# Attention steps between dependent hops, relus between projection chunks, and filter loads on another queue, in a four-layer convolution and attention kernel

## The chip, the cores and the metric

The kernel runs on one core of a Trainium2 chip, in one launch. The metric is device microseconds of that core for one execution of the whole program: the median of three runs. The engines are named as the profile names them: PE is TensorE (PEld its weight loads), ACT is ScalarE, DVE is VectorE, POOL is GpSimd and SP is SyncE, which here only issues DMAs.

## The reference

Four layers act on x of shape 4 x 256 x 64 x 64 (images, channels, rows, columns), all in 32-bit floats. Each adds its result to a normalised input:

```python
def _L0_conv_ref(x, ...):                 # non-local block
    xs = conv3x3(x, smooth_w) + smooth_b
    xs = relu(group_norm(xs, gn1_w, gn1_b))           # 8 groups
    g_x, theta_x, phi_x = conv1x1(xs, ...)            # 128 channels each, 4096 tokens
    attn = softmax(einsum('bnc,bcm->bnm', theta_x, phi_x))
    y = einsum('bnm,bmc->bnc', attn, g_x)
    w_y = group_norm(conv1x1(y, w_w, w_b), gn2_w, gn2_b)
    return w_y * 0.1 + xs
def _L1_conv_ref(x, ...):                 # linear attention, 4 heads of 32
    q, k, v = conv1x1(rmsnorm(x), w_qkv)
    q, k = softmax(q, axis=-2), softmax(k, axis=-1)
    context = einsum('bhdn,bhen->bhde', k, v)
    out = einsum('bhde,bhdn->bhen', context, q * scale)
    return rmsnorm(conv1x1(out, w_out) + b_out)
def _L2_conv_ref(x, ...):                 # generated depthwise 3x3 and pointwise kernels
    dk, pk = gen_kernel(x, Wd1, ...), gen_kernel(x, Wp1, ...)
    return pointwise(depthwise3x3(x, dk), pk) + bias
def _L3_conv_ref(x, ...):                 # mixture of four 1x1 experts, gated by the pooled input
    return conv1x1(x, mixture(experts, gate(x)))

for L in (_L0_conv_ref, _L1_conv_ref, _L2_conv_ref, _L3_conv_ref):
    x = x + L(_gn(x))                     # group norm, 32 groups
```

## The kernel before, in words

The 256 channels are two halves (`h`, NH = 2) of 128 partitions; an image's 4096 pixels lie along the free axis, in chunks of CH = 1024 or 512 columns.

**Stages.** The images b = 0 to 3 go through in overlap. The first convolution runs (`convolve_first`), and `project` turns image 0's relu output `big` into phi, theta and g (the tile `tpg`). In stage b, for b = 0, 1, 2, the attention over image b (`attend(b)`) is interleaved with other layers: in stage 0 with the preparation of the convolution's weights and the convolution of image 1 (`convolve_second`), in stages 1 and 2 with all that is left of image b - 1 after its attention (`tail(b - 1)`) and with the convolution of image b + 1 (`convolve`). Then `project` runs for image b + 1, with only the finish of the last attention block beside it. Stage 3 interleaves `attend(3)` with `tail(2)`; `tail(3)` comes last, alone.

**Attention steps.** `attend` has 128 steps per image. One step issues two products of logits (`pf`, L989), their exponentials on ScalarE (`pr`, L990), and two products of the probabilities before it into `py` (L1097); eight matmul instructions of 128 x 512 in all. Logits run one step ahead of the products that use them.

**Chain and credit.** The order on every engine is written out by hand (`manual_schedule`), and each engine works its queue in that order. A layer is a Python generator that issues some instructions and yields a cost n. `Chain.steps` adds n times the stage's rate (1.22 in stage 0, 0.86 in stages 1 and 2, 1.24 in stage 3) to a credit; for each whole unit it lets one attention step be issued and then whatever `w.later` has put off by so many steps. So whether a step falls between two hops of a layer depends on the credit at that point. The final `tail(3)` has a chain of its own (`end`), which draws on work held back for it.

**Hops.** `group_finish` (L339) is the finish of a group norm: statistics on VectorE (`mv`), an averaging matmul (`pm`, L351), `ev` on VectorE, a second matmul (`pv`, L366), then the reciprocal root. It is called in `nonlocal_out`, `input_stats`, `normed_relu`, `linear_attention`, `generated` and `mixed`. `linear_attention` (L1214) scales chunks of its input with `normed` (half 0 on ScalarE, L1234, half 1 on VectorE, L1235), transposes them on TensorE (`turned`, `ps_xt`, L1246), and after its chunks goes through `cx`, `cxT`, `cmT`, `w2`, each a small matmul and a copy. `generated` (L1432) makes the depthwise kernels for the taps on VectorE (L130); `mixed` gates the experts (`ps_hid`, L1708).

**Relus.** `normed_relu` (L666) ends a convolution: `group_finish`, then relu over `big` on ScalarE: eight activations of 128 x 1024 (L687), or for image 1, whose result lies in a planar layout, sixteen of 128 x 512 that read it transposed (L676). Each region is added to `xs_d` in DRAM, which `copy_x` has filled with the input, by an accumulating DMA from GpSimd (`add_by_dma`).

**Filters.** The convolutions are done as products with transformed filters. `load_filter` (L478) fetches one of 256 KB to a `u` tile (three buffers) from `filters` or `rows_d`, one product ahead, all on SyncE's queue; `convolve` makes 24 products per image, `convolve_second` 18 pairs. SyncE also issues the images' loads, `copy_x`, the loads and stores of the attention's results, and the gather of `inv` (L1022).

Of the kernel before, what the change touches and what calls it, by code (L numbers as in the profile page):

```python
# [10 lines left out]
ALU = mybir.AluOpType  # L11
# [35 lines left out]
class Chain:  # L47
# [46 lines left out]
def conv_preact_fast(ctx: ExitStack, tc: tile.TileContext, guard, x, wc, wtpg, ww, wqkv, wout, w1cat, wd2,  # L94
# [244 lines left out]
    def group_finish(st, avg, eps, shift=None, between=()):  # L339

        mv, late = st() if callable(st) else aggregated(st), None
        if isinstance(mv, tuple):
            mv, late = mv
        if shift is not None:
            tt(mv[:, :, 0], mv[:, :, 0], shift, ALU.add)
        yield 1
        pm = bank("pm")  # L350
        nc.tensor.matmul(pm[:, 0:NH], avg, mv[:, :, 0], start=True, stop=True)  # L351
# [12 lines left out]
        yield 1  # L364
        pv = bank("pv")
        nc.tensor.matmul(pv[:, 0:NH], avg, ev, start=True, stop=True)  # L366
# [111 lines left out]
    def load_filter(a, k, last):  # L478

        u = filter_tile("u")  # L480
        nc.sync.dma_start(out=u, in_=rows_d[a, :, :, 0 if k == 0 else 2] if k in (0, last) else filters[a, :, k - 1])
        return u

    def joining(a, y, t):
# [178 lines left out]
        for h in range(NH):  # L663
            nc.sync.dma_start(out=xs_d[b, h], in_=x[b, bass.ts(h, P), :])

    def normed_relu(w, b, st):  # L666
# [4 lines left out]
        if b == 1:  # L671
            for s in range(2):
                tiles = bass.ts(s, IY // 2)
                for h in range(NH):
                    for k in range(MY):
                        nc.scalar.activation(  # L676
                            image[:, h, tiles, k, :].rearrange("p i (t j) -> p i j t", j=MX),
                            outs[:, h, k].rearrange("p j (i t) -> p i j t", t=IX)[:, tiles], AF.Relu,
                            bias=sh[:, h:h + 1], scale=sc[:, h:h + 1])
                        yield 0.5  # L680
                    cols = bass.ts(s, N // 2)
                    w.later(1, lambda h=h, cols=cols: add_by_dma(xs_d[b, h, :, cols], big[:, h, cols]))
            return
        for c in range(N // CH):
            cols = bass.ts(c, CH)
            for h in range(NH):
                nc.scalar.activation(big[:, h, cols], big[:, h, cols], AF.Relu, bias=sh[:, h:h + 1], scale=sc[:, h:h + 1])  # L687
                w.later(1, lambda h=h, cols=cols: add_by_dma(xs_d[b, h, :, cols], big[:, h, cols]))
                yield 0.3

    def convolve(w, b):

# [56 lines left out]
            yield 0.8  # L749
        yield from w.pending()  # L750
        stats(3)
        yield from normed_relu(w, b, st)

    def convolve_second(w):

        _, gm, rstd = yield from input_stats()
        yield from normalise_planar(gm, rstd)
        st = stats_tile()
        products, joined, rows_joined, joining, stats = planar_joiner(st)
        PRODUCTS = [(a, pair) for a in range(TY) for pair in PAIRS]  # L760
# [12 lines left out]
        def join(a, pair, ps):  # L773
            dst = joined(a, pair, ps, False)
            if pair == (3, 4):
                if a == 5:
                    some(len(rest))
                w.later(1, lambda: joined(a, pair, ps, True))
            elif pair == (1, 2):
                pass  # L780
            elif a == 4:

                for oh in range(NH):
                    rest.extend(joining(a, oh, dst[oh]))
                for j in range(4):
                    w.later(1 + j, lambda: some(3))
                for j in range(3):
                    w.later(5 + j, lambda j=j: stats(j))
            elif a == 2:
                for oh in range(NH):  # L790
                    rest.extend(joining(a, oh, dst[oh]))
                for j in range(3):
                    w.later(1 + j, lambda: some(2))
            else:
                some(len(rest))
                for oh in range(NH):
                    w.later(1, lambda oh=oh: rows_joined(a, oh, dst[oh]))

        def load_filters(i):
            a, pair = PRODUCTS[i]  # L800
            return [load_filter(a, k, 5) for k in pair]

        us = load_filters(0)
        copy_x(1)
        for i, (a, pair) in enumerate(PRODUCTS):
            if pair == PAIRS[0]:

                pace = 1.8 if a == 5 else 0.87
                for op, *args in down(a, planar, ra, rt, ra):
                    op(*args)  # L810
                    yield 0.75 * pace
            (v, ops), u = across(pair), us
            if i + 1 < len(PRODUCTS):
                us = load_filters(i + 1)
            for op, *args in ops:
                op(*args)
                yield 0.4 * pace
            w.later(1, lambda a=a, pair=pair, v=v, u=u: multiply(a, pair, v, u))
            yield pace
        yield from w.pending()  # L820
        stats(3)
        yield from normed_relu(w, 1, st)

    def convolve_first(w):

# [90 lines left out]
            tt(mean, mean, minus, ALU.subtract)  # L916
            return mv

        yield from normed_relu(w, 0, moments)


    def project():

        for c in range(N // 512):
# [194 lines left out]
    def nonlocal_out(w, b, big, k4, xs_in):  # L1119
# [94 lines left out]
    def linear_attention(w, b, big, qT, k4, st, sh, sums):  # L1214
# [16 lines left out]
        def normed(c):  # L1231
            cols = bass.ts(c, 512)
            xg = k4("xg").rearrange("p (h n) -> p h n", h=NH)
            nc.scalar.activation(xg[:, 0, :], big[:, 0, cols], AF.Identity, bias=nb[:, 0:1], scale=rstd[:, 0:1])  # L1234
            nc.vector.tensor_scalar(xg[:, 1, :], big[:, 1, cols], rstd[:, 1:2], nb[:, 1:2], ALU.mult, ALU.add)  # L1235
            return xg

        def turned(xg):
# [97 lines left out]
        yield 1  # L1336
# [5 lines left out]
        yield 1  # L1342

        pw = bank("ps_w2")
        nc.tensor.matmul(pw[:, 0:NH * P], cmT, wout_s, start=True, stop=True)
# [3 lines left out]
        yield 1  # L1349

        st = stats_tile()

# [77 lines left out]
    TAPS = [(i, j) for i in range(3) for j in range(3) if (i, j) != (1, 1)]  # L1430

    def generated(w, b, big, k4, st, sh, diag):  # L1432
        mv, gm, rstd = yield from group_finish(st, avg8, 1e-5, sh)

        pivot = sp.tile([P, NH], F32, name="pivot", bufs=1)
# [397 lines left out]
    with tc.manual_schedule(engines={E.PE, E.Activation, E.DVE, E.Pool, E.SP}):  # L1833
        run(Chain(convolve_first).steps())
        run(project())
        for b in range(B - 1):
# [609 lines left out]
```

## Time and profile before

| | |
|---|---|
| median of three runs | 3051.3 us (3050.59 to 3051.98) |
| the profiled execution, own time | 3047.78 us |
| its span | 3045.6 us |
| its mean granted clock | 0.991 |
| PE busy | 2950.2 us, 97% |
| DVE busy | 2062.9 us, 68% |
| ACT busy | 1189.3 us, 39% |
| POOL busy | 130.6 us, 4% |
| attention products (L989 and L1097), PE | 970.8 + 963.5 us |
| DMA moved | 200.55 MB, mean 66 GB/s |

The profile is of one execution. Busy times of the engines overlap. A row of groups has, after the bar, the busy time of all its instructions and the mean of one in ns, then the idle time before them and what ended it. A line of the timeline has the start in us, the duration, the engine, the line of the code, the operation and its tiles, how many instructions it sums (x8), and in brackets the idle time ahead and what ended it.

### The profile page before, as it was taken

How to read it: one execution, taken by the hardware profiler on the slowest of the kernel's cores; microseconds unless marked ns; L12 is line 12 of the kernel's file. 1: busy time of each engine (PE TensorE's matmuls, PEld its weight loads, DVE VectorE, ACT ScalarE, POOL GpSimd, SP SyncE). 2: the span in 40 equal slices, each digit the busy share in tenths (PEclk: the TensorE clock that was granted, in tenths of full speed). 3: DMA queues.
4: the chain of work that ended last, by engine and by line, in shares of the span. 5: the costliest groups of instructions: out<-in, count | busy, mean ns of one | idle time of the engine just before them, and what ended most of it. 6: DMA issues, size and time to landing. Idle time of an engine off the chain costs nothing.

```text
span 3045.6 us, 24705 instructions
## 1 busy us (share of the span) xinstructions
PE 2950.2 (97%) x8562; PEld 1497.6 (49%) x8562; DVE 2062.9 (68%) x2842; ACT 1189.3 (39%) x2295; POOL 130.6 (4%) x178
## 2 busy tenths in 40 slices
PE   6899999999999999999999999999999999999998
PEld 3454555445664444444566444444446544444743
DVE  8747677853646994777545797568554559876584
ACT  2234333353555333223365532412335453333632
POOL 0100000000011000001011000000100100000100
PEclk9999999999999999999999999999999999999998
DMA  5234434352113233532410433333422222234021
GB/s 222 76 104 98 104 55 47 42 70 81 57 8 47 27 76 76 111 52 58 132 7 11 54 20 87 134 50 45 103 84 14 25 42 38 36 90 92 22 69 67
DMA packets 532389, 200.55 MB, mean 66 GB/s; under 512 B 470689, under 2 KB 480673, under 8 KB 528033
## 3 DMA queue, kind: packets, MB, share of 16 engines
q1 hardware_dynamic: 528224, 182.12, 29.2%
q0 software_dynamic: 4032, 16.78, 3.0%
q8 instruction: 69, 1.13, 0.2%
q14 instruction: 64, 0.52, 0.1%
HBM read 130.13 MB, written 85.52 MB: 71 GB/s over the span
## 4 chain that ended last, share of the span: by engine, by line
PE 84%; DVE 8%; issue 5%; DMA 2%; ACT 1%; POOL 0%; SPq 0%; DVEq 0%; POOLq 0%; ACTq 0%
PE pf L989 26%; PE py L1097 26%; PE ps_conv L515 4%; PE ps_tp L929 4%; PE ps_qk L1266 3%; PE ps_ex L1754 3%; PE ps_pw L1532 3%; PE ps_conv L587 2%; PE ps_g L934 2%; PE ps_ctx L1293 2%; PE ps_wy L1041 2%; PE ps_o L1359 2%; PE ps_dw L1579 1%; DVE big L130 1%; DMA u<-filters 1%
## 5 line engine op out<-in xcount | busy, mean ns | idle before, releaser
L990 ACT ACTIVATE pr<-pf 128x512 f32<-128x512 f32 x1024 | 605.2, 597 | 1096.8 <-PE pf L989 1045.5
L989 PE MATMUL pf<-tpg 128*128 128x512 f32 x2048 | 970.8, 597 | 0.0
L1097 PE MATMUL py<-pr,tpg 128*128 128x512 f32 x2048 | 963.5, 593 | 3.8 <-ACT pr L990 3.6
L127 DVE TENSOR_TENSOR tot<-tot,pr 128x1024 f32<-128x1024 f32 x448 | 546.6, 1220 | 225.9 <-ACT pr L990 225.0
L1097 PEld LDWEIGHTS py<-pr,tpg 128*128 128x128 f32 x2048 | 389.8, 190 | 496.7 <-issue 483.0
L989 PEld LDWEIGHTS pf<-tpg 128*128 128x128 f32 x2048 | 385.5, 191 | 432.5 <-issue 411.5
L130 DVE SCALAR_TENSOR_TENSOR dw<-xp,dk,dw 128x1008 f32<-128x1008 f32 x208 | 262.8, 1267 | 6.5 <-ACT dw L1524 3.6
L515 PE MATMUL ps_conv<-v,u 128*128 128x512 f32 x384 | 174.6, 602 | 7.4 <-DMA u<-rows_d 4.6
L515 PEld LDWEIGHTS ps_conv<-v,u 128*128 128x128 f32 x384 | 73.9, 193 | 102.5 <-issue 100.6
L929 PE MATMUL ps_tp<-big,wtpg_s 128*128 128x512 f32 x256 | 117.2, 601 | 3.0 <-ACT big L687 3.0
L127 DVE TENSOR_TENSOR tpg<-ps_g,bg_s 128x512 f32<-128x512 f32 x32 | 22.1, 691 | 143.5 <-PE ps_g L934 143.5
L220 POOL TENSOR_TENSOR rstd<-rstd,half 128x2 f32<-128x2 f32 x24 | 17.5, 729 | 2324.2 <-DVE rstd L368 2207.6
L1266 PE MATMUL ps_qk<-wqkv_s,xg 128*128 128x256 f32 x496 | 113.7, 379 | 0.0
L1266 PEld LDWEIGHTS ps_qk<-wqkv_s,xg 128*128 128x128 f32 x496 | 93.9, 190 | 23.3 <-issue 12.0
L1532 PE MATMUL ps_pw<-dw,pk 128*128 128x512 f32 x216 | 97.4, 592 | 0.0
L930 ACT ACTIVATE tpg<-ps_tp,btp_s 128x512 f32<-128x512 f32 x64 | 43.8, 686 | 116.8 <-PE ps_tp L929 116.6
L1281 DVE TENSOR_REDUCE qs<-qk 128x16 f32<-128x512 f32 x25 | 17.1, 686 | 86.2 <-ACT qk L1276 86.2
L929 PEld LDWEIGHTS ps_tp<-big,wtpg_s 128*128 128x128 f32 x256 | 47.6, 194 | 54.5 <-issue 50.0
L1276 ACT ACTIVATE qk<-ps_qk,rinv 128x256 f32<-128x256 f32 x100 | 47.2, 474 | 67.7 <-PE ps_qk L1266 64.6
L934 PEld LDWEIGHTS ps_g<-wtpg_s,big 128*128 128x128 f32 x512 | 62.2, 192 | 15.3 <-issue 15.3
L127 DVE TENSOR_TENSOR v<-ra 128x1024 f32<-128x1024 f32 x58 | 69.2, 1220 | 0.3
L1762 ACT ACTIVATE res<-ps_ex,b 128x512 f32<-128x512 f32 x56 | 38.1, 687 | 77.8 <-PE ps_ex L1754 75.9
(390 smaller groups left out, 3079.0 us busy)
## 6 DMA issues: line engine op xcount, KB each, us to landing
xp<-in_x_dram SPq DMA_DIRECT2D x16, 1024.0 KB, 8.2
wy_d<-wt SPq DMA_DIRECT2D x32, 512.0 KB, 3.0
wy<-wy_d SPq DMA_DIRECT2D x32, 512.0 KB, 4.9
out_dram<-res SPq DMA_DIRECT2D x64, 256.0 KB, 2.0
xs_d<-big POOLq DMA_DIRECT2D x24, 512.0 KB, 11.9
u<-filters SPq DMA_DIRECT2D x48, 256.0 KB, 3.1
xs<-xs_d SPq DMA_DIRECT2D x24, 512.0 KB, 5.7
u<-rows_d SPq DMA_DIRECT2D x36, 256.0 KB, 3.2
```

What stands on the lines that cost most here:

```text
L127: nc.vector.tensor_tensor(o, a, b, op)
L130: nc.vector.scalar_tensor_tensor(o, a, s, b, op0, op1)
L515: nc.tensor.matmul(ps[oh], u(oh, h), v[:, bass.ts(h, 512)], start=(h == 0), stop=(h == NH - 1))
L587: nc.tensor.matmul(ps[:, bass.ts(oh, IY * IX)], u[i][:, h, bass.ts(oh, P)], v[:, i, bass.ts(h, IY * IX)], start=(h == 0), stop=(h == NH - 1))
L929: nc.tensor.matmul(ps, wtpg_s[:, h, k, :], big[:, h, cols], start=(h == 0), stop=(h == NH - 1))
L934: nc.tensor.matmul(ps[:, j, :], big[:, h, bass.ts(4 * c + j, P)], wtpg_s[:, h, 2, :], start=(h == 0), stop=(h == NH - 1))
L989: nc.tensor.matmul(pf, phi[:, bass.ts(2 * m + s, P)], theta[:, bass.ts(q, 512)], start=True, stop=True)
L990: nc.scalar.activation(pr[:, bass.ts(s, 512)], pf, AF.Exp)
L1097: nc.tensor.matmul(py, g[:, bass.ts(2 * m + s, P)], probs[i][:, bass.ts(s, 512)], start=(m == 0 and s == 0), stop=(m == NM - 1 and s == 1))
L1266: nc.tensor.matmul(ps[:, 0:2 * HID], xg[:, h, bass.ts(j, P)], wqkv_s[:, h, 0:2 * HID], start=(h == 0), stop=(h == NH - 1))
L1532: nc.tensor.matmul(ps, pk[:, h * NH * P + oh * P:h * NH * P + (oh + 1) * P], dw[h][:, bass.ts(s, 512)], start=(h == 0), stop=(h == NH - 1))
L1754: nc.tensor.matmul(ps, wm[h][:, bass.ts(oh, P)], big[:, h, bass.ts(c, 512)], start=(h == 0), stop=(h == NH - 1))
```

## The change

1. A layer may yield `None`. That issues exactly one attention step at that place and takes one from the credit, to which the rate is added: the average pace stays, and the place is fixed. It stands at both hops of `group_finish`, before the `group_finish` of `nonlocal_out` and of `generated` (except in the last tail), before that of the relus in `convolve` and `convolve_second`, after the first relus, between `normed(0)` and the first transposes of `linear_attention` (except in the last tail), and at the four hops from `cx` to the outputs.
2. `normed_relu` cuts its relus in eight pieces (a 1024-column chunk of one half; for image 1 a piece is four activations of 128 x 256). Two run at once. The other six wait in a list, and `project` takes one after each of its 512-column chunks. The accumulating DMA is issued with its piece.
3. `convolve` (images 2 and 3) loads its filters from ScalarE's queue.
4. `convolve_second` loads the first filter of the next pair before, and the second after, the product of a pair.
5. In the last tail, `normed` does half 1 on ScalarE as well for every chunk but the first, and two products instead of one are issued ahead.
6. The rates become 1.34, 0.845 and 1.2.

```diff
@@ Chain.steps
             for n in part:
+                if n is None:
+                    credit += self.rate - 1
+                    yield
+                    self.tick()
+                    continue
                 credit += n * self.rate
@@ group_finish (both hops)
-        yield 1
+        yield None
         pm = bank("pm")
...
-        yield 1
+        yield None
         pv = bank("pv")
@@ load_filter
-        nc.sync.dma_start(out=u, in_=...)
+        (nc.scalar if last == 3 else nc.sync).dma_start(out=u, in_=...)
@@ normed_relu
+    relus = []
+    def normed_relu(b, st, hops=0):
         bias = vec_s[:, V_SB, :]
+        for _ in range(hops):
+            yield None
         _, gm, rstd = yield from group_finish(st, avg32, 1e-5, bias)
         sc, sh = affine(gm, rstd, vec_s[:, V_G1W, :], vec_s[:, V_G1B, :], bias, 1.0)
+        def piece(c, h):
             cols = bass.ts(c, CH)
+            if b == 1:
+                tiles = bass.ts(c, IY // 4)
+                for k in range(MY):
+                    nc.scalar.activation(
+                        image[:, h, tiles, k, :].rearrange("p i (t j) -> p i j t", j=MX),
+                        outs[:, h, k].rearrange("p j (i t) -> p i j t", t=IX)[:, tiles], AF.Relu,
+                        bias=sh[:, h:h + 1], scale=sc[:, h:h + 1])
+            else:
                 nc.scalar.activation(big[:, h, cols], big[:, h, cols], AF.Relu, bias=sh[:, h:h + 1], scale=sc[:, h:h + 1])
-                w.later(1, lambda h=h, cols=cols: add_by_dma(xs_d[b, h, :, cols], big[:, h, cols]))
-                yield 0.3
+            add_by_dma(xs_d[b, h, :, cols], big[:, h, cols])
+        relus.extend(lambda c=c, h=h: piece(c, h) for c in range(N // CH) for h in range(NH))
+        for _ in range(NH):
+            relus.pop(0)()
+        yield None
@@ convolve, convolve_second: the relus' own first None
-        yield from normed_relu(w, b, st)
+        yield from normed_relu(b, st, 1)
@@ convolve_second
-        def multiply(a, pair, v, u):
+        def multiply(a, pair, v, u, after):
             ps = products(pair, v, u)
+            after()
...
-            (v, ops), u = across(pair), us
-            if i + 1 < len(PRODUCTS):
-                us = load_filters(i + 1)
+            (v, ops), u, us = across(pair), us, []
+            load_one(us, i + 1, 0)
...
+            w.later(1, lambda a=a, pair=pair, v=v, u=u, after=lambda us=us, i=i: load_one(us, i + 1, 1): multiply(a, pair, v, u, after))
@@ project, after each chunk
+            if relus:
+                relus.pop(0)()
             yield
@@ nonlocal_out
+        else:
+            yield None
         wmv, gm, rstd = yield from group_finish(wy_stats[b], avg32, 1e-5, bias, between)
@@ linear_attention
-            nc.scalar.activation(xg[:, 0, :], big[:, 0, cols], AF.Identity, ...)
-            nc.vector.tensor_scalar(xg[:, 1, :], big[:, 1, cols], ...)
+            for h in range(NH):
+                if h == 1 and (c == 0 or not alone):
+                    nc.vector.tensor_scalar(xg[:, h, :], big[:, h, cols], ...)
+                else:
+                    nc.scalar.activation(xg[:, h, :], big[:, h, cols], AF.Identity, ...)
...
         xg, first = normed(0), ()
+        if not alone:
+            yield None
         rinv, banks = turned(xg)
         if alone:
-            first = [product(xg, 0)]
+            first = [product(xg, j) for j in range(2)]
...
@@ linear_attention, at each of four hops (cx, cxT, cmT, w2)
-        yield 1
+        yield None
@@ generated
+        if diag is None:
+            yield None
         mv, gm, rstd = yield from group_finish(st, avg8, 1e-5, sh)
@@ the stages
-            run(Chain(both(*parts), 1.22 if b == 0 else 0.86).steps(), attention)
+            run(Chain(both(*parts), 1.34 if b == 0 else 0.845).steps(), attention)
-        run(Chain(tail(B - 2, big, qT, held=held), 1.24).steps(), attention)
+        run(Chain(tail(B - 2, big, qT, held=held), 1.2).steps(), attention)
```

More of the change, by code (lines that the diff above doesn't have):

```diff
@@ L480, in load_filter @@
         u = filter_tile("u")
-        nc.sync.dma_start(out=u, in_=rows_d[a, :, :, 0 if k == 0 else 2] if k in (0, last) else filters[a, :, k - 1])
+        (nc.scalar if last == 3 else nc.sync).dma_start(out=u, in_=rows_d[a, :, :, 0 if k == 0 else 2] if k in (0, last) else filters[a, :, k - 1])
         return u
@@ L664, in copy_x @@
             nc.sync.dma_start(out=xs_d[b, h], in_=x[b, bass.ts(h, P), :])
-    def normed_relu(w, b, st):
+    relus = []
+    def normed_relu(b, st, hops=0):
         bias = vec_s[:, V_SB, :]
+        for _ in range(hops):
+            yield None
         _, gm, rstd = yield from group_finish(st, avg32, 1e-5, bias)
         sc, sh = affine(gm, rstd, vec_s[:, V_G1W, :], vec_s[:, V_G1B, :], bias, 1.0)
[L671 to L681, printed above, removed]
-                    w.later(1, lambda h=h, cols=cols: add_by_dma(xs_d[b, h, :, cols], big[:, h, cols]))
-            return
-        for c in range(N // CH):
-            cols = bass.ts(c, CH)
-            for h in range(NH):
-                nc.scalar.activation(big[:, h, cols], big[:, h, cols], AF.Relu, bias=sh[:, h:h + 1], scale=sc[:, h:h + 1])
-                w.later(1, lambda h=h, cols=cols: add_by_dma(xs_d[b, h, :, cols], big[:, h, cols]))
-                yield 0.3
+        def piece(c, h):
+            cols = bass.ts(c, CH)
+            if b == 1:
[6 more added lines that the diff above has]
+            else:
+                nc.scalar.activation(big[:, h, cols], big[:, h, cols], AF.Relu, bias=sh[:, h:h + 1], scale=sc[:, h:h + 1])
+            add_by_dma(xs_d[b, h, :, cols], big[:, h, cols])
[3 more added lines that the diff above has]
+        yield None
     def convolve(w, b):
@@ L797, in join, with load_one @@
                     w.later(1, lambda oh=oh: rows_joined(a, oh, dst[oh]))
[L799 to L803, printed above, removed]
+        def load_one(us, i, n):
+            if i < len(PRODUCTS):
+                a, pair = PRODUCTS[i]
+                us.append(load_filter(a, pair[n], 5))
+        us = []
+        for n in range(2):
+            load_one(us, 0, n)
         copy_x(1)
@@ L817, in convolve_second @@
                 yield 0.4 * pace
-            w.later(1, lambda a=a, pair=pair, v=v, u=u: multiply(a, pair, v, u))
+            w.later(1, lambda a=a, pair=pair, v=v, u=u, after=lambda us=us, i=i: load_one(us, i + 1, 1): multiply(a, pair, v, u, after))
             yield pace
@@ L821, in convolve_second @@
         stats(3)
-        yield from normed_relu(w, 1, st)
+        yield from normed_relu(1, st, 1)
     def convolve_first(w):
@@ L917, in moments @@
             return mv
-        yield from normed_relu(w, 0, moments)
+        yield from normed_relu(0, moments)
     def project():
@@ L1233, in normed @@
             xg = k4("xg").rearrange("p (h n) -> p h n", h=NH)
-            nc.scalar.activation(xg[:, 0, :], big[:, 0, cols], AF.Identity, bias=nb[:, 0:1], scale=rstd[:, 0:1])
-            nc.vector.tensor_scalar(xg[:, 1, :], big[:, 1, cols], rstd[:, 1:2], nb[:, 1:2], ALU.mult, ALU.add)
+            for h in range(NH):
+                if h == 1 and (c == 0 or not alone):
+                    nc.vector.tensor_scalar(xg[:, h, :], big[:, h, cols], rstd[:, h:h + 1], nb[:, h:h + 1], ALU.mult, ALU.add)
+                else:
+                    nc.scalar.activation(xg[:, h, :], big[:, h, cols], AF.Identity, bias=nb[:, h:h + 1], scale=rstd[:, h:h + 1])
             return xg
@@ L1335, in linear_attention @@
         nc.scalar.copy(cxT, pt[:, 0:NH * P])
-        yield 1
+        yield None
         pe = bank("ps_cm")
@@ L1341, in linear_attention @@
         tt(cmT, pe[:, 0:P], avg32, ALU.mult)
-        yield 1
+        yield None
         pw = bank("ps_w2")
@@ L1348, in linear_attention @@
         w.settle()
-        yield 1
+        yield None
         st = stats_tile()
@@ L1432, in generated @@
     def generated(w, b, big, k4, st, sh, diag):
+        if diag is None:
+            yield None
         mv, gm, rstd = yield from group_finish(st, avg8, 1e-5, sh)
```

## The prediction

> **What bounds the kernel now.** I read the page first, then busy time by stretch, the waits of TensorE by stretch, the timeline around each wait, and the groups.
>
> ```profile
> PE 2950.2 (97%) x8562; PEld 1497.6 (49%) x8562; DVE 2062.9 (68%) x2842; ACT 1189.3 (39%) x2295; POOL 130.6 (4%) x178
> PE   6899999999999999999999999999999999999998
> PEclk9999999999999999999999999999999999999998
> ```
>
> TensorE is busy 97%: only about 95 us of the span are idle, and no matmul is removed. By stretch:
>
> ```profile
> 745.00:1440.00 695.00, 680.70 (x1882) 334.29 (x1881) 495.99 (x659) 274.35 (x534) 34.82 (x41) 0.99 0.30 56
> 1485.00:2180.00 695.00, 680.69 (x1882) 334.43 (x1882) 496.48 (x660) 274.06 (x534) 34.83 (x41) 0.99 0.30 56
> ```
>
> The second number is TensorE's busy time. These are the stages of attention on images 1 and 2 (stages 1 and 2 below), each with 14.3 us idle and the same waits, so every figure for one counts twice. The other stretches: the head to 26 us, 24.6 idle; the first projection, 8.4 (relus, untouched); stage 0 (185 to 745), 0; stage 3 (2224 to 2795), 2.3; the tail after 2795, about 36 with the image-3 layers alone. TensorE's waits from 745 to 1485 (columns: total us, times, longest):
>
> ```profile
> PE pm L351 <- DVE mv L127: 5.3, 3, 3.0
> PE ps_conv L515 <- DMA u<-rows_d: 2.3, 1, 2.3
> PE ps_xt L1246 <- ACT xg L1234: 2.1, 1, 2.1
> PE py L1097 <- ACT pr L990: 1.8, 1, 1.8
> PE ps_conv L515 <- DMA u<-filters: 1.4, 1, 1.4
> PE pv L366 <- DVE ev L127: 0.8, 1, 0.8
> PE ps_w L1345 <- DVE cmT L127: 0.4, 1, 0.4
> ```
>
> The sum is 14.1: this list is what the change can win in a stage. A wait also slows what follows, or doesn't:
>
> ```profile
> 789.78 1.25 PE L1246 MATMUL ps_xt<-ident,xg 128*128 128x128 f32 x8 [2.13 <-ACT xg L1234]
> 790.83 3.46 PE L989 MATMUL pf<-tpg 128*128 128x512 f32 x4
> ...
> 1529.61 1.10 PE L1246 MATMUL ps_xt<-ident,xg 128*128 128x128 f32 x8 [2.13 <-ACT xg L1234]
> 1530.54 1.88 PE L989 MATMUL pf<-tpg 128*128 128x512 f32 x4
> ```
>
> After the same 2.13 us gap four matmuls took 3.46 us once and 1.88 once. That extra (1.58) is the clock.
>
> **Removed, step by step.** One attention step is 3.43 us of TensorE. The hops that now wait had no step between them, or one too early; a demanded step covers any hop in the list, the longest being 2.98.
> - Head of the non-local block, pm 1.58 x 2 = 3.2; generated kernel, pm 0.70 x 2 + 0.19 in stage 3 = 1.6; statistics before the relus, pm 2.98 x 2 = 6.0; input statistics, pv 0.84 x 2 = 1.7. First transposes, 2.13 x 3 = 6.4; context chain (ps_w), 0.38 x 2 = 0.8.
> - Exps behind four relus in a row: 1.81 x 2 = 3.6. Two relus (2.3 us) now stand ahead of them, about what a step leaves ScalarE free (3.43 less two exps of 0.6).
> - Filters: (1.38 + 2.33) x 2 = 7.4. The cause is SyncE's queue (the view after the next sums).
> Idle time: 30.7. Clock: matmuls after these gaps against the undisturbed 1.88 (four) and 3.60 (eight convolution matmuls): 1.58 after the transposes, 1.77 and 1.68 after the filters (5.37 and 5.28), 1.51, 1.88 and 1.02 after the relus' statistics: 9.4.
>
> ```profile
> 1241.87 0.37 SPq L1022 DMA_DIRECT2D inv<-sum_d  x1
> 1242.35 8.62 SPq L481 DMA_DIRECT2D u<-rows_d  x1
> 1254.17 5.37 PE L515 MATMUL ps_conv<-v,u 128*128 128x512 f32 x8 [2.33 <-DMA u<-rows_d]
> ```
>
> The filter's issue stood 8.62 us on SyncE, behind the gather of `inv`; elsewhere an issue takes 0.33 to 0.52 and a filter lands in 3.2 (median). The first wait is a load issued at 1225.86 behind copy_x, 15.3 us to landing. From ScalarE the loads stand behind neither.
>
> In the tail's linear attention both halves of `normed` go to ScalarE after chunk 0, and two products stand ahead:
>
> ```profile
> PE ps_xt L1246 <- DVE xg L1235: 3.9, 2, 2.4
> ```
>
> The two waits are 1.47 and 2.39. VectorE gets 0.54 us back per chunk, ScalarE takes 0.82 more on some 4.9 of a 6.5 us chunk, so it keeps up. I put the first at 0.5 (the second product, two 0.38 matmuls, fills it) and the second at 0: 3.4 won (bounds: -1 to 3.9, if ScalarE were late with its second half).
>
> Gains: 30.7 + 9.4 + 3.4 = 43.5.
>
> **Added.**
>
> ```profile
> L687 ACT ACTIVATE big<-big,sh,sc 128x1024 f32<-128x1024 f32 x24 | 28.0, 1235 | 12.7 <-DVE sh L127 12.7
> L676 ACT ACTIVATE big<-xp,sh,sc 128x512 f32<-128x512 f32 x16 | 19.7, 1312 | 2.9 <-DVE sh L127 2.9
> L1234 ACT ACTIVATE xg<-big,nb,rstd 128x512 f32<-128x512 f32 x24 | 19.6, 816 | 6.1 <-DVE nb L127 5.7
> ```
>
> - Image 1's relus (transposed reads). Contiguous rows give 0.82 ns per element and 0.40 us fixed (816 and 1235 ns); the transposed 512 take 1312. With the fixed part kept, 256 take 0.86 alone; half of 1312 is 0.66; I take 0.77. Two pieces are then eight activations, 6.2 us, ahead of the exps. Four relus of 4.64 us made py wait 1.81, so 6.2 makes it wait 3.4 (2.6 to 4.1). The other six pieces (3.1 each) fall one into each chunk of the projection, which is 5.22 us on TensorE. A piece whose half completes a 1024-column tile is needed two matmul groups later: it is ready about 4.05 after the previous theta activation, TensorE wants it at 2.64: 1.45 x 3 = 4.4 (3.0 to 5.3). Sum 7.8 (5.6 to 9.4). The relus on image 1 were spread over attention steps before, and stage 0 had no wait, so nothing excludes this loss. Images 2 and 3: a piece is 1.15, ready at 2.1 of 2.64, hidden by the projection's matmuls; uncovered it would be 1.2 x 3 per image.
> - A step moves away from one hop. Replaying the credit at both rates, the demanded steps give every listed hop at least one, but in stages 1 and 2 the hop from pv to ps_hid (the experts' gate) falls from one step to none. The nearest row is that wait in the tail, alone:
>
> ```profile
> 3000.44 0.59 PE L1708 MATMUL ps_hid<-rpool,rw_s 128*64 128x1 f32 x4 [1.23 <-DVE rpool L127]
> ```
>
>  TensorE's order is fixed, so the attention's matmuls behind it wait too: 1.2 x 2 = 2.4 (0 to 3).
> - Filter loads on ScalarE: 12 at 0.33 and 12 at 0.52 is 10.2 us a stage, on an engine busy 274 of 695. Behind each stand the next exps, for which TensorE waits; a step has 3.43 - 1.2 = 2.2 us of slack on ScalarE, so one issue hides. The first filter now stands behind the normalising activations, and beside copy_x: 0 to 4.5, and I take 2.0 x 2 = 4.0.
> - Exps behind three of those activations in a row (1.24 each; four of 1.16 cost 1.81): 0.5 x 2 = 1.0 (0 to 1.8).
> - Rate 0.86 to 0.845 gives VectorE more work per step in the depthwise taps, where it is busy 49.4 of 50: 0.5 for both (0 to 2.6). Otherwise the rates cost nothing: steps per image stay 128, and by the replay 126, 126 and 121 are used (124, 127, 120 before). If they ran out, each bare hop would cost 1 to 3.
> - Clock after the new waits, two of them as above: 2 x 1.65 = 3.3 (0 to 6).
> - Accumulating DMAs issued at once on GpSimd (0.88 each, engine 4% busy) are read a stage later: nothing. The second filter of each pair in convolve_second moves behind the multiply; its cover is two attention steps (6.9 us) against 3.2 to land; without it each of 36 loads could cost some us.
>
> Costs: 7.8 + 2.4 + 4.0 + 1.0 + 0.5 + 3.3 = 19.0. Net 43.5 - 19.0 = 24.5. The profiled execution took 3047.8 (span 3045.6), 3.5 under the median of 3051.3; it would become 3023.3, the median **3026.8**.
>
> **Two rules against the trace.** The row: 2.13 us idle, then 3.46 for 1.88. The Trainium skill, "TensorE: Matmul & The Clock Gate", Part 1, "The HAM clock gate", lets the clock drop only after about 3.4 us of idleness. By it no gap here costs clock: gains 34.1, costs 15.7, net 18.4, 3032.9. The trace differs, in five of the gaps; I take the trace, and keep the rule in the range. Second, 8.62 us of held issue. "DMA: Bandwidth & Descriptors", "Issuing engines are not separate DMA queues", says all issuers share the same 16 DMA engines and only issue time is saved. By it the transfers of copy_x and `inv` would delay a filter from ScalarE as well, and 7.4 + 3.45 (their clock) are not won: 24.5 - 10.9 = 13.6, 3037.7. I take the 8.62, which is issue time, but not as certain.
>
> **Rivals.**
> - R1, the costs hide: relus' waits and the first filter prove covered, net about -40, 3011. For: TensorE had no wait in stage 0, with the same relus. Against: eight in a row precede one pair of exps. 0.18.
> - R2, filters gain nothing (the shared engines): 3037.7, as above. For: 15.3 us beside copy_x. Against: 8.62 is issue. 0.20.
> - R3, slower: filter loads hold ScalarE's queue. A load waits for its tile, three of them, while exps stand behind. At 1 us per load, 48 loads make +48: about 3075. It decides at 24.5 / 48 = 0.51 us per load. For: SyncE was held 8.62 once. Against: 2.2 us of slack per step. 0.05.
> - Not doing what it says: where credit already gave a step (stage 0 and 3), a demanded one changes nothing, and the gaps could move to the next hop; no measurable change 0.05.
>
> **How the numbers follow.** The forecast has 0.52; with all costs at their low ends it is 3013, with all at their high ends 3040; they won't all lie on one side, so its own range is 3016 to 3036. Adding R1 and most of R2: 3010 to 3042. This kernel's measurement tells about 0.2%, 6 us. Faster 0.52 + 0.18 + 0.20 = 0.90; within, 0.05; slower, R3, 0.05.
>
> **What would show it.** In stages 1 and 2: pm, ps_xt and py waits gone, TensorE idle near 7 instead of 14.3; a new ps_hid wait of 1.2; no filter issue over 1 us. In the projection of image 1, which ends near 745: ps_tp waiting on relus about 1.45, three times, and py 3.4 before it. Wrong: py waits spread over stages 1 and 2 (R3), or filters still waited for behind copy_x (R2).

## The result, and the profile after

The changed kernel takes 3042.36 us (median of 11 runs, 3041.30 to 3044.86) against 3050.06 for the kernel before in the same runs: a ratio of 0.9978, 95% interval 0.9969 to 0.9987. It is faster by about 7 us; the prediction said 24.5. The profiled execution took 3041.82, 5.96 less than the one before.

The page after, the same three lines:

```profile
PE 2948.7 (97%) x8562; PEld 1496.9 (49%) x8562; DVE 2057.4 (68%) x2835; ACT 1192.6 (39%) x2318; POOL 122.0 (4%) x182
PE   6899999999999999899999999999999999999998
PEclk9999999999999999999999999999999999999999
```

At this resolution nothing has happened but an 8 in one slice, 1216 to 1292 us, where the first of the waits below lies. The stretches of stages 1, 2 and 3 (they start and end at other times now; the second number is TensorE's busy time, the first the length):

```profile
750.00:1437.00 687.00, 675.29 (x1888) 333.04 (x1887) 495.39 (x659) 266.07 (x529) 22.73 (x35) 1.00 0.30 56
1480.00:2172.00 692.00, 680.20 (x1899) 335.83 (x1898) 496.52 (x660) 267.04 (x530) 22.73 (x35) 0.99 0.30 56
2214.00:2786.00 572.00, 569.14 (x1636) 286.22 (x1635) 384.78 (x542) 244.46 (x496) 24.61 (x29) 0.99 0.30 51
```

Stages 1 and 2 still have 11.7 and 11.8 us idle, where 14.3 were before and about 7 were forecast. In the whole execution TensorE's idle time fell from 95.4 to 91.3 us and its busy time by 1.5. The waits of TensorE from 745 to 1485 show that it is other idle time (total, times, longest):

```profile
PE ps_conv L520 <- DMA u<-filters: 7.6, 1, 7.6
PE pm L356 <- DVE mv L132: 2.3, 1, 2.3
PE ps_hid L1730 <- DVE rpool L132: 1.2, 1, 1.2
PE ps_zt L1409 <- DVE z L132: 0.6, 1, 0.6
```

Of the seven waits of before none is left at its place, as forecast. But one filter alone now costs twice what two did, and a hop that had no wait (the group norm ahead of linear attention) has one of 2.3. In the projection of image 1:

```profile
PE ps_tp L940 <- ACT big L686: 2.0, 3, 0.7
PE py L1110 <- ACT pr L1003: 2.0, 1, 2.0
```

The timeline where the 7.6 arises (ACTq is ScalarE's own DMA queue), and the line of the tile's transfers:

```profile
1225.45 1.31 SPq L669 DMA_DIRECT2D xs_d<-in_x_dram  x2
1226.36 0.35 ACTq L486 DMA_DIRECT2D u<-filters  x1
...
1242.81 5.07 PE L520 MATMUL ps_conv<-v,u 128*128 128x512 f32 x8 [7.57 <-DMA u<-filters]
...
DMA to landing us min/median/max: 3.0/7.0/16.3
```

The first filter is issued 0.9 us after the 4 MB of copy_x and lands 16.3 us later. The eight matmuls then take 5.07 instead of 3.60. Before, SyncE's order put the first filter ahead of copy_x, and only the second stood behind; the first product waited for nothing:

```profile
1223.83 0.46 SPq L481 DMA_DIRECT2D u<-filters  x1
1224.34 1.48 SPq L664 DMA_DIRECT2D xs_d<-in_x_dram  x2
1225.86 0.58 SPq L481 DMA_DIRECT2D u<-filters  x1
...
1232.89 3.60 PE L515 MATMUL ps_conv<-v,u 128*128 128x512 f32 x8
```

Stage 3 has a wait that it did not have, and its cause is in these lines:

```profile
2531.23 0.37 SPq L1035 DMA_DIRECT2D inv<-sum_d  x1
2531.64 9.06 SPq L1479 DMA_DIRECT2D wp<-in_wp_dram  x2
...
2544.22 0.75 DVE L135 SCALAR_TENSOR_TENSOR pk<-wp,pb,pk 128x512 f32<-128x512 f32 x1 [11.20 <-DMA wp<-in_wp_dram]
...
2546.20 2.06 ACT L1003 ACTIVATE pr<-pf 128x512 f32<-128x512 f32 x4 [7.41 <-DVE tot L132]
2546.85 3.78 PE L1110 MATMUL py<-pr,tpg 128*128 128x512 f32 x4 [2.86 <-ACT pr L1003]
2550.43 3.13 PE L1002 MATMUL pf<-tpg 128*128 128x512 f32 x4
```

Behind the gather of `inv` the two issues of `wp` take 9.06 us on SyncE, the first of them 8.6. In stages 1 and 2 the gather used to meet a filter; now, in stage 3, it meets `wp`. VectorE waits 11.2 us for it, ScalarE's exps wait 7.41 us for VectorE to read the exps before them (`tot`), and TensorE waits 2.86 and then takes 3.78 and 3.13 us for four matmuls instead of 1.88.

### The profile page after: what moved, and what is told of

It reads as the page before. It is cut to its first block, busy times and chain, and to the rows that moved or that the text cites. A ratio compares the mean times of both kernels' runs of the same rounds, so it can differ in the third digit from the quotient of the medians.

```text
span 3040.0 us, 24678 instructions
## 1 busy us (share of the span) xinstructions
PE 2948.7 (97%) x8562; PEld 1496.9 (49%) x8562; DVE 2057.4 (68%) x2835; ACT 1192.6 (39%) x2318; POOL 122.0 (4%) x182
## 4 chain that ended last, share of the span: by engine, by line
PE 70%; DVE 3%; DMA 1%; issue 1%; ACT 1%; POOL 0%; POOLq 0%; DVEq 0%; ACTq 0%
PE pf L1002 20%; PE py L1110 20%; PE ps_conv L520 6%; PE ps_ex L1776 4%; PE ps_qk L1284 3%; PE ps_pw L1554 3%; PE ps_tp L940 3%; PE ps_ctx L1311 2%; PE ps_o L1379 2%; PE ps_dw L1601 1%; PE ps_g L945 1%; PE ps_wy L1054 1%; DMA u<-filters 1%; PE ps_xt L1264 1%; PE ps_zt L1409 1%
## 5 line engine op out<-in xcount | busy, mean ns | idle before, releaser
L132 DVE TENSOR_TENSOR tot<-pr 128x1024 f32<-128x1024 f32 x32 | 39.1, 1222 | 55.6 <-ACT pr L1003 46.8
L945 PEld LDWEIGHTS ps_g<-wtpg_s,big 128*128 128x128 f32 x512 | 62.2, 192 | 15.3 <-issue 15.3
```

Of the source, the lines that this page charges most:

```text
L132: nc.vector.tensor_tensor(o, a, b, op)
```

## The experiments

Each was timed in five rounds or more beside the kernel before; the ratio is to that kernel. The changed kernel stands at 0.9978.

**1, 2, 3. Where the first filter is issued.**

```diff
# 1: first two from SyncE, ahead of copy_x; the others stay on ScalarE
-        us = load_filters(0)
+        us = [load_filters(0), load_filters(1)]
         copy_x(b)
# 2: the same two on ScalarE's queue, ahead of normalise()
# 3: all on SyncE, one ahead, as before the change
-        (nc.scalar if last == 3 else nc.sync).dma_start(out=u, ...)
+        nc.sync.dma_start(out=u, ...)
```

> The changed kernel, but the first two filters of convolve are loaded from SyncE's queue ahead of copy_x; the other 22 stay on ScalarE's. Theory A (the first filter is late because its transfer was issued behind the 4 MB of copy_x and shares the 16 DMA engines with it): TensorE's waits for u<-filters, 7.6 us in each of stages 1 and 2, go, and with them the slower matmuls behind them (5.1 instead of 3.6 us): 2 x 9.1 = 18 us less than the changed kernel, about 3024. Theory B (the loads from ScalarE's queue are dear in themselves, behind exps and activations): the waits move to the third filter, less than 5 us won.

> The changed kernel, but the first two filters are issued on ScalarE's queue before the normalising activations, so ahead of copy_x in time; all 24 stay on ScalarE's queue. Theory A (order against copy_x): as with SyncE, 18 us less than the changed kernel, about 3024. Theory B (ScalarE's queue is what makes them late): the waits of 7.6 us stay in good part, over 3035.

> The changed kernel with all filters back on SyncE's queue, as before the change. Theory A: the first filter is again issued ahead of copy_x, so the 7.6 us waits go (18 us with the clock); the second stands behind copy_x again (1.4 in each stage), and where the gather of inv holds SyncE's queue for 8.6 us a filter may be caught again (2.3 and 1.7 of clock in each stage): 7 to 15 us less than the changed kernel, 3027 to 3035. Theory B' (part 3 of the change is neutral, the loss is elsewhere): within 3 us of the changed kernel.

Measured: 3033.11 (0.9945, 0.9932 to 0.9959), 3033.65 (0.9947, 0.9934 to 0.9961), 3032.08 (0.9945, 0.9931 to 0.9958). The filter wait is gone in all three, whichever queue issues: order against copy_x is the cause (theory A), not ScalarE's queue (B). Only 9 to 10 us came back of the 18 expected in 1 and 2, since another wait stood behind: VectorE's `v`, the product's other operand. The timeline of the first, and TensorE's wait in the whole of it:

```profile
1226.17 1.35 SPq L486 DMA_DIRECT2D u<-filters  x2
1227.57 1.19 SPq L669 DMA_DIRECT2D xs_d<-in_x_dram  x2
...
1239.06 3.70 PE L520 MATMUL ps_conv<-v,u 128*128 128x512 f32 x8 [3.10 <-DVE v L132]
...
PE ps_conv L520 <- DVE v L132: 6.2, 2, 3.1
```

**4. `wp` from ScalarE's queue** (`nc.scalar.dma_start(out=t, in_=wp2...)`).

> The changed kernel with the weights wp of the generated pointwise kernel loaded from ScalarE's queue (16 loads). Theory C (in stage 3 the gather of inv held the next load on SyncE, wp, for 8.6 us; VectorE waited 11 us for it, ScalarE for the buffers that VectorE had not freed, TensorE 2.9 us for the exps, and four matmuls then took 3.8 instead of 1.9): TensorE's py wait of 2.86 in stage 3 goes, 4.8 us less than the changed kernel, about 3037.5. Theory D (VectorE falls behind because the rate of stage 3 was lowered from 1.24 to 1.2): the wait stays, no change.

3040.23 (0.9969, 0.9957 to 0.9982): 2 us rather than 4.8 in the median, and the interval overlaps the changed kernel's, so the time does not settle it. The profile does: stage 3 has no wait of TensorE left, at the same rate of 1.2. The place of `wp` behind the gather is the cause (C), not the rate (D); the fifteenth experiment, which moves the gather instead of `wp`, removes the same wait.

**5, 6. Steps and rates.**

```diff
# 5: the first experiment's kernel with
         yield from normalise(gm, rstd)
+        yield None
# 6: the changed kernel with
-  1.34 if b == 0 else 0.845 ... 1.2
+  1.34 if b == 0 else 0.86 ... 1.24
```

> The first experiment's kernel (first two filters ahead of copy_x) with one more demanded step in convolve, after the normalising activations. There TensorE waited 3.1 us per stage for VectorE's v, with one attention step fewer between pv and the first product than before the change (3 instead of 4). Theory E (a demanded step is taken out of the credit, so the hop behind goes without; the steps are moved, not added): one step of 3.4 us in front, less its 1.2 us on VectorE, leaves about 0.9 of each 3.1: 4.4 us less, 6 with the clock, about 3028. Rival F (VectorE has too much work there, steps or not): the wait stays, 3033.

> The changed kernel with the rates of stages 1 to 3 as before (0.86, 0.86, 1.24); stage 0 keeps 1.34. Theory D (the lower rates let VectorE fall behind): the pm wait of 2.28 us before linear attention in stages 1 and 2 and the py wait of 2.86 in stage 3 go, with their clock about 9 us less than the changed kernel, 3033. Theory E (where the demanded steps fall, not the rates, makes these waits): pm stays within 1 us of 2.28; the py wait of stage 3 goes only if the gather no longer stands ahead of wp: 0 to 5 us less, 3037 to 3042.

The fifth: 3030.24 (0.9938, 0.9925 to 0.9952), 3 us less than the first where 4.4 to 6 were expected; the `v` wait falls from 3.1 to 1.4 and a py wait of 1.1 comes. So a step in front takes more than half of that wait (E), though not all; the times of the two kernels are not told apart by their intervals.

The sixth: 3031.31 (0.9941, 0.9927 to 0.9954), 11 us less than the changed kernel, more than either theory had. Its waits of TensorE from 1150 to 1440, for 7.6 and 1.2 of the changed kernel:

```profile
PE ps_conv L520 <- DMA u<-filters: 3.5, 1, 3.5
PE pss L1070 <- DVE inv L1066: 1.8, 1, 1.8
PE ps_log L1737 <- DVE hb L1734: 0.6, 1, 0.6
```

Two things moved with the rate. With the old one there are four attention steps between `pv` and the first product, not three, so that product finds its `v` ready. And SyncE now issues copy_x only behind the store of `inv` (in the changed kernel it went out 15 us before that store), so the first filter, issued from ScalarE, is ahead of it by 0.5 us:

```profile
1234.88 0.35 ACTq L486 DMA_DIRECT2D u<-filters  x1
1235.04 0.33 SPq L1033 DMA_DIRECT2D sum_d<-inv  x1
1235.42 1.19 SPq L669 DMA_DIRECT2D xs_d<-in_x_dram  x2
1236.59 0.33 ACTq L486 DMA_DIRECT2D u<-filters  x1
...
1241.54 3.60 PE L520 MATMUL ps_conv<-v,u 128*128 128x512 f32 x8
...
1252.03 9.78 PE L520 MATMUL ps_conv<-v,u 128*128 128x512 f32 x16 [3.46 <-DMA u<-filters]
```

The first filter lands in 2.9 us and the first product does not wait; the second, behind copy_x, lands in 15.3, and the second product waits 3.46. Both come from the same queue, so this is theory A again, the order against copy_x, and here nobody planned it. The ps_hid wait goes, and the py wait of stage 3 too (`wp` was held 6.2 us there, and no wait of TensorE came of it), while new waits of 7.0 us in all come at pss, ps_xt and ps_log. The pm wait of 2.28 stays; the seventh and the thirteenth, with the demanded steps alone, have it at the new rates and at the old. So it is the demanded steps' own (E).

**7, 13. The demanded steps alone**, in the kernel before: at the new rates of stages 1 to 3, and at the old.

> The kernel before, with part 1 of the change alone: the demanded steps and the rates of stages 1 to 3; relus, filters and the tail as before, and stage 0 at its old rate of 1.22. Prediction's sum: 19.7 of idle time in hops (head, transposes, context, generated, pv, relu statistics) and 6.0 of clock, less 2.4 for ps_hid and 0.5: about 3027. Theory E adds what the changed kernel showed: pm 2.3, v 3.1 and pv 0.5 in each of stages 1 and 2, 4.8 in stage 3, less the filters' 7.4 and their clock 3.45 if the gather no longer meets a filter: 3050 - 22.8 + 11.8 + 4.8 - 10.9 = about 3033; 3044 if it still does.

> The kernel before with the demanded steps alone and all rates as before; the seventh experiment's kernel with 0.86 and 1.24 for 0.845 and 1.2. Rates theory: the seventh's v waits (6.2), ps_hid (2.4) and stage 3's 1.9 go, with the clock 12 us less than its 3041.6: about 3030. If the gather of inv meets a filter on SyncE's queue as in the ninth (10 us a stage there), all of that is lost again: 3045 to 3050.

3041.62 (0.9973, 0.9962 to 0.9984) and 3047.96 (0.9990, 0.9983 to 0.9996). The seventh is well above its 3033, although no filter is waited for: the exps now stand behind six relus in a row (6.9 us), not four, and py waits 3.9 there in each of stages 1 and 2, not 1.8. That is 4.2 of the 8.6 us, and the slower matmuls behind it are about 3 more (eight took 6.25 us in stage 1 and 5.4 in stage 2, instead of 3.60). The thirteenth is the worse of its two cases: TensorE waits 13 us in each stage for a filter:

```profile
1229.33 1.19 SPq L669 DMA_DIRECT2D xs_d<-in_x_dram  x2
1230.61 0.53 SPq L1029 DMA_DIRECT2D inv<-sum_d  x1
1231.19 20.95 SPq L486 DMA_DIRECT2D u<-filters  x1
```

The steps moved copy_x and the gather together; the gather, right behind copy_x, holds the next filter for 21 us. The same rates that won 11 us in the sixth lost 5 to 6 here. So a rate has no price of its own here: it decides what falls where on the queues.

**8. Filters from ScalarE alone**, in the kernel before.

> The kernel before, with part 3 alone: convolve's filters from ScalarE's queue. Theory A (order against copy_x): the first filter is issued about 1 us behind copy_x, lands 16 us later, about 8 us after TensorE wants it, in each of stages 1 and 2, and the waits of 1.38 and 2.33 go: (8 - 3.7) x 2 = 8.6 slower than before, about 3058. The prediction's sum (waits of 7.4 and clock of 3.45 go, 4.0 for the first filter): 7 us faster, about 3043.

3057.81 (1.0028, 1.0018 to 1.0038): slower, as theory A had it. (That the median meets 3058 is luck: the nine runs lie between 3054 and 3064, and the profiled one is the slowest.) Part 3 of the change is a loss taken alone:

```profile
1225.46 1.32 SPq L664 DMA_DIRECT2D xs_d<-in_x_dram  x2
1226.14 0.36 ACTq L481 DMA_DIRECT2D u<-filters  x1
...
1242.56 5.75 PE L515 MATMUL ps_conv<-v,u 128*128 128x512 f32 x8 [7.88 <-DMA u<-filters]
```

**14. The relus alone** (part 2 in the kernel before).

> The kernel before with part 2 alone: relus in eight pieces, two at once and six between the projection's chunks, one demanded step after the first two. By the rows: exps behind four relus, 1.81 in each of stages 1 and 2, go; image 1 adds 1.98 and 3 x 0.67, as measured in the changed kernel: 3.6 - 4.0, nothing, within 3 us of before. The prediction's sum had 3.6 won and 7.8 lost: 4 us slower.

3050.49 (1.0004, 0.9996 to 1.0012): no difference, as the rows had it, with the same 1.98 and 3 x 0.67 for image 1 as in the changed kernel.

**9, 11. The gather.** The ninth has the old rates and all filters on SyncE, two ahead; the eleventh adds

```diff
             nc.sync.dma_start(out=sum_d[at], in_=inv)
             yield
-            nc.sync.dma_start(out=inv..., in_=sum_d[at]...)
-            for _ in range(6):
+            yield
+            nc.scalar.dma_start(out=inv..., in_=sum_d[at]...)
+            for _ in range(5):
```

> The changed kernel with the old rates of stages 1 to 3 (as in the sixth experiment) and all filters on SyncE's queue, the first two ahead of copy_x. Theory A and the rates (each removes its own waits): of the sixth's waits, u<-filters 7.4 goes with about 3 of clock: 3021. Rival G (the two fixes remove the same wait, since with the old rates the first product comes a step later): no more than 3 us below the sixth, over 3028.

> The ninth, with the gather of inv (16,384 pieces) issued from ScalarE's queue, one step later after its store; ScalarE issues no other DMA then. Theory C (the gather holds the next DMA of the queue that issued it, for 8.5 us): the issues of 8 to 10 us on SyncE in stages 1 to 3 go, and no wait of TensorE on u, wp or out follows: 0 to 6 us below the ninth. Rival H (what holds SyncE is the 16 engines being full, whoever issues): the issues of 8 us stay on SyncE. Risk: ScalarE waits for the store to land, and TensorE for exps: up to 28 x 1 us more.

The ninth: 3045.33 (0.9986, 0.9978 to 0.9993), 14 us worse than the sixth, which neither theory had. The gather stands right behind copy_x again. SyncE, and TensorE's wait from 1225 to 1275:

```profile
1236.12 1.19 SPq L669 DMA_DIRECT2D xs_d<-in_x_dram  x2
1237.41 0.55 SPq L1035 DMA_DIRECT2D inv<-sum_d  x1
1238.00 21.59 SPq L486 DMA_DIRECT2D u<-rows_d  x2
...
PE ps_conv L520 <- DMA u<-rows_d: 10.1, 1, 10.1
```

The eleventh: 3026.41 (0.9918, 0.9905 to 0.9932), 19 us less than the ninth. No single issue on SyncE takes over 1.9 us any more, where the next one behind a gather took up to 21 in the ninth, and the filter waits fall from 20.6 to 3.4 in all. By rival H the holds would have stayed on SyncE.

**15, 16. The gather on ScalarE's queue**, in the changed kernel (whose filters are there too) and in the kernel before (no other DMA there).

> The changed kernel with the gather of inv on ScalarE's queue, where its filters stand too. Theory C (the gather holds the next DMA of the queue that issued it): a filter's issue stands 8 us on ScalarE where one follows a gather, with exps behind it, and TensorE waits for py or ps_conv: in stages 1 and 2 some 5 us each more, while stage 3 loses its wait (4.8 less): about 3047. If the hold is not bound to the queue: 3038.

> The kernel before with nothing changed but the gather of inv: on ScalarE's queue (no other DMA there), one step later. Theory C: SyncE's 8.6 us holds go, and with them TensorE's wait for u<-rows_d (2.33 in each of stages 1 and 2) and its clock (1.7 each): 8 us faster than before, 3042. If not bound to the queue: no change.

The sixteenth: 3041.34 (0.9967, 0.9955 to 0.9979), 9 us less than before for one moved DMA. On SyncE no issue takes over 1.5 us; before, 13 took 3.7 to 9.3. This is what ties the hold to the queue. That the time meets C's 8 is in part luck, for TensorE's waits are not as C had them:

```profile
PE py L1098 <- ACT pr L990: 5.1, 3, 1.8
PE ps_conv L515 <- DMA u<-filters: 4.6, 2, 2.4
```

The wait for u<-rows_d (4.6 in all) is gone, but py waits 1.5 more than before and u<-filters, behind copy_x, 1.8 more. The profiled execution is 5.96 us shorter, and 4.0 of that is TensorE's busy time, for the same matmuls: clock.

The fifteenth: 3039.74 (0.9963, 0.9949 to 0.9976), not slower as expected, and not told apart from the changed kernel. Its stage 3 has no wait. On ScalarE two filters followed a gather by 6.9 us and were held 2.2 each; all others came later and were not held. So there the hold met nothing that mattered, and what it does to a DMA right behind it on ScalarE was not seen.

**10, 12. Towards a better kernel**: the ninth and the eleventh with a step ahead of linear attention's group norm, a step between image 1's first two relus, and the six later relus behind phi's activation.

> The ninth, with a demanded step before the group norm of linear attention (pm waits 2.28 us per stage there), a step between image 1's first two relus (py waited 1.98), and the six later relus set one matmul group earlier in each chunk, after phi's activation (ps_tp waited 0.67 three times). Prediction by the rows: 4.6 + 2.0 + 2.0 = 8.6, about 10 with the clock, below the ninth: 3011. Rival F (VectorE is what is late at pm: 3.76 us of work per step of 3.43): a step gives 3.43 less its own 1.22, so the wait falls to about 0.1; if the step is taken from another hop, only 4 us are won.

> The tenth and the eleventh together. If they remove different waits the gains add up: about 3008; if the moved gather shifts other transfers into new waits, between the two.

3044.94 (0.9979, 0.9971 to 0.9986), no gain on the ninth where 10 us were expected, and **3024.82** (0.9915, 0.9901 to 0.9928), the lowest median of all, 1.6 us under the eleventh and not told apart from it; 3008 was expected. The pm wait ahead of linear attention, image 1's ps_tp waits and 0.7 of its py wait went; waits of 1.2 to 2.1 came at ps_b, ps_hid, ps_wy and ps_tp. The steps were moved, not added.

## Why the prediction was wrong, point by point

The terms of its sum, against the profile (us of TensorE, + is won):

| term | forecast | measured |
|---|---|---|
| hops: head, transposes, context, generated, pv, relu statistics | +19.7 | +14.0 |
| exps behind four relus | +3.6 | +3.6 |
| filters' waits, with the first filter's cost | +7.4 - 4.0 | -7.7 |
| tail's transposes | +3.4 | +2.5 |
| image 1's relus | -7.8 | -4.0 |
| ps_hid | -2.4 | -2.5 |
| exps behind normalising | -1.0 | 0 |
| rates, VectorE's lag | -0.5 | -2.9 |
| clock, net | +6.1 | +1.8 |
| sum | 24.5 | 4.8 |

The profiled executions differ by 5.96 us; 0.8 of the 1.2 that the terms leave over is two waits of pm in the last tail (0.52 and 0.31) that went without being in the forecast.

- **The step that failed first is the filters.** The prediction said that from ScalarE the loads stand behind neither copy_x nor the gather, and put the first filter, issued beside copy_x, at 2.0 a stage (bounds 0 to 4.5); it is 7.6. It had the row that says so: a filter behind copy_x takes 15.3 us to land. It treated the queue's order only as a hindrance, and did not see that the same order had kept the first filter ahead of copy_x. 11.1 of the 18.5 us missing are here. Experiments 1 to 3 and 8 show the cause; undoing it returned 9 to 10 us, because `v` was late as well. Rival R2, the shared engines, was right in kind and too mild: the filters did not gain nothing, they lost. The skill's other rule that spoke against this change ("DMA: Bandwidth & Descriptors", "Issuing engines are not separate DMA queues") held for copy_x, by the 16.3 us, and not for the gather's hold, which went with the queue (experiment 16).
- **The hops** themselves went as forecast; all the waits listed are gone. What was missing is the other side of an average that stays: new waits at pm ahead of linear attention, 2.28 and 2.35, and 0.55 twice at ps_zt. The prediction had replayed the credit and counted every hop with at least one step as covered. This one was not, because VectorE was behind:

```profile
790.24 1.22 DVE L132 TENSOR_TENSOR tot<-tot,pr 128x1024 f32<-128x1024 f32 x1
791.38 1.28 DVE L1223 BATCH_NORM_STATS2 st<-big 128x6 f32<-128x512 f32 x2
792.58 0.58 DVE L341 BATCH_NORM_AGGREGATE mv<-st 128x2 f32<-128x48 f32 x2
793.40 0.38 PE L356 MATMUL pm<-mv,avg 128*128 128x2 f32 x2 [2.28 <-DVE mv L132]
793.65 1.96 PE L1002 MATMUL pf<-tpg 128*128 128x512 f32 x4
```

VectorE works there without a gap: from 779.69 to 790.24 three rounds of `tot`, `st` and `big`, 3.52 us each, against 3.43 of TensorE's step. A step demanded at this place removes the wait (the tenth).
- **Rates "cost nothing" was wrong.** The prediction put 0.5 on them, for VectorE. The lower rates took a step from the first product and one from ps_hid, let copy_x go out ahead of the first filter, and put the hold of `wp` in stage 3 where TensorE waits for it (2.86, in the table under rates, and 3.15 of clock); the sixth experiment undoes all four. The thirteenth shows the opposite sign with filters on SyncE.
- **Right:** ps_hid (1.23 twice), the exps behind relus, that filter issues hide in ScalarE's slack (R3 did not come: no spread of py waits), the 8.6 us as an issue's hold and not the transfer's (experiments 11 and 16). But it took the hold for a single case, with issues of 0.33 to 0.52 elsewhere; there were 13, eleven of them of 8.5 to 9.3.
- **Too dear:** image 1's relus. Eight in a row took 5.05 us and four 2.63, so 0.63 to 0.66 each, not 0.77; ps_tp waited 0.67 three times for 1.45 forecast.
- **Clock:** the rule of the Trainium skill that the trace outweighed ("TensorE: Matmul & The Clock Gate", Part 1, "The HAM clock gate", idleness of about 3.4 us) is contradicted again: after 2.35 us idle at 1525, four matmuls took 3.45 instead of 1.96. But after 2.28 at 793 (above) they took 1.96.

```profile
1525.49 0.58 PE L356 MATMUL pm<-mv,avg 128*128 128x2 f32 x2 [2.35 <-DVE mv L132]
1525.93 3.45 PE L1002 MATMUL pf<-tpg 128*128 128x512 f32 x4
```

What failed is that new, longer gaps brought their own clock loss: 1.47 and 1.52 after the filters, 1.5 at 1525, and 1.9 and 1.25 in stage 3, 7.6 where 3.3 were put.

Left open: why the clock drops after some gaps of 2.3 us and not after others, and how much of the moved steps a rate between the two would give back. Parts 4 and 5 and the rate of stage 0 were not run alone; for part 5 the profile has the 2.5 us of the table, and stage 0 has no wait of TensorE before or after.

## What to carry to other kernels

An order on one queue does two things: it delays what stands behind, and it protects what stands ahead. Before moving a DMA to another queue, list what it was ahead of, above all the large transfers, and place it ahead of them by hand. A step demanded at one place under a fixed average is taken from another, so list the hops that had one to spare; and look for the one transfer that holds a queue (here the gather) and move that, rather than all that suffers from it.

## What the runs showed of the hardware that was not expected

- A gather of 16,384 pieces of 16 bytes takes 0.4 us to issue, but the next DMA on the same queue is held until about 10 us after it: held 8.5 to 9.3 us if it comes within 1.4 us, 3.7 and 4.0 if after 6.3, and not at all after 19 or more (in the kernel before eleven, two and fifteen cases). Issued right behind copy_x, it held the next one 21 us (the ninth and the thirteenth). With the gather moved to ScalarE's queue, the holds left SyncE (the eleventh and the sixteenth).
- ScalarE's queue issues a DMA ahead of the work that stands before it: the first filter is behind four normalising activations in program order, was issued at 1226.36, and the last of them ended at 1231.4 (the changed kernel; in stage 2 the same, 1960.11 and 1965.1). The logits (`pf`) that the exps ahead of it wait for were done at 1226.31, so it seems that only the waits in front delayed it; that was not tested.
- Activations that read transposed cost nearly by the element when back to back: four of 128 x 256 took 2.63 to 2.65 us (the changed kernel), two of 128 x 512 took 2.38 to 2.40 (the kernel before).
